# A decoder layer over 32 sequences: the order of TensorE's steps in an attention round, wide score passes first, and a selection cut into four parts

## The chip, the cores and the metric

The kernel runs on one core of one Trainium2 chip. The metric is the device time in microseconds of one execution. Three executions of the kernel before took 3460.85, 3463.48 and 3466.79 us; their median is 3463.48 us.

A core has five engines that run side by side, each through its own queue: TensorE (matmuls and transposes through PSUM; PE in the profile, with its weight loads shown as PEld), VectorE (DVE), ScalarE (ACT), GpSimd (POOL) and SyncE (SP, here the engine that issues nearly all DMAs).

## The reference

The input is 32 sequences of 256 tokens with 256 features, and for each a context of 120 rows with 256 features. Three blocks follow one another, each as x = layernorm(x + block(x)).

- Latent self-attention. A token is projected to a latent of 72 numbers, which is key and value for all 16 heads. Each head projects the token to a query of 72. The scores q·k/4 are masked causally, go through a softmax, and weigh the latents. The 16 results of 72 are put together (1152 numbers) and projected to 256.
- Cross-attention with 16 heads of 64 over the context: queries from x, keys and values from the context, softmax, output projection.
- A mixture of experts with a shared expert. A gate of 16 experts gives each token a softmax. Each expert takes the 32 highest-scored tokens of each sequence, applies a gated unit with a hidden width of 512 and adds its output, times the score, to these tokens. A shared unit of the same form runs over all tokens.

All arrays are float32.

```
scores = einsum('bhtl,bsl->bhts', q, Wdkv) / 4          # causal mask, softmax, then
y      = einsum('bhts,bsl->bhtl', attn, Wdkv)           # z @ out_w + out_b
logits = einsum('bthk,bfhk->bhft', k, q)                # cross attention, softmax, v, Wo
topk_w, topk_idx = top_k(softmax(x @ gate_w.T).T, 32)   # per sequence and expert
```

## The kernel before

**Two stages.** The attention stage does both attention blocks, sequence by sequence, in 32 calls of `attention_round(n)` (line 790). A stage of experts follows (`feed_forward`, line 1048), in whose first part the last steps of attention are mixed. The change lies in the attention stage, apart from two lines of the second.

**A round is a pipeline over sequences.** Round n works on the latent attention of sequence n, on the end of that of n-1, on the cross-attention of n-1 and n-2, on the routing of n-3, and prepares n+1. It has four sections, 0 to 3. Each begins with `scores(n, g)` (line 401) for one group g of four heads.

**Scores.** A head's 72 query numbers are split into 64 and 8. The 8s of four heads lie side by side in one tile, 32 rows a head, so `scores` runs four matmuls at a time in 32-row tiles of the array (line 410). Then the 64s of two heads run at a time in 64-row tiles (line 422). The scores of a head fill one PSUM bank of 384 columns: 128 for the first half of the tokens (the narrow pass, t = 0, which needs the first 128 keys only) and 256 for the second half (the wide pass, t = 1). A float32 matmul appears as two instructions in the profile. Afterwards VectorE adds the causal mask, which copies the scores from the bank into the tile `sm` (line 431) and frees the bank.

**Softmax and turning.** `weights(n, g, t)` (line 434) takes maxima on VectorE, four exponentials on ScalarE, reciprocals on VectorE and the product on GpSimd (line 455). `turns` transposes the weights in three steps k of four blocks (`turn`, line 457), into the banks pT; k = 0 and 2 are copied out by ScalarE, k = 1 by VectorE. A section turns the weights of the group before it: `turns(n, g-1)`, and section 0 `turns(n-1, 3)`.

**Weighing.** `weigh(s, g)` (line 480) multiplies the turned weights with the 64-wide part of the values, in tiles of 64 columns. `weigh_rest` (line 503) does the 8-wide rest of all heads in tiles of 32 columns. `latent_out` (line 520) projects to 256, adds x and normalizes.

**Cross-attention.** `cross_keys`, `cross_values` and `cross_queries` (lines 541 to 587) are projections with all 128 rows. `cross_scores(s, c0, t)` (line 589) uses 64-row tiles and fills both banks of the kind "l". `cross_weights` is the softmax over them, `cross_turn` transposes, `cross_weigh` (line 630) works in 64-column tiles, and `cross_out` (line 652) projects, adds, normalizes and stores.

**PSUM.** Of the eight banks, two have the tag "l" and six the tag "r" (`BUFS`, line 127). All other steps take an "r" bank when they begin. A new allocation takes the bank of the sixth allocation before it, and the matmul waits until that bank's reader is done. `scores` takes four banks at once.

**Routing and selection.** Every four sequences `route` and `score` compute the gate. Every eight sequences `select(g)` (line 731), at the end of section 3 of rounds 10, 18 and 26 and once in the stage of experts, transposes the scores of eight sequences by 16 experts to 128 rows of 256, and finds the 32 highest in each row. It does so four times over: the eight highest (`max`, line 745), their positions (`max_index`, line 746), and their replacement by -1 (`match_replace`, line 748). At the end of the next round `place` turns the positions into offsets.

**What sets the order.** In rounds 1 to 31 TensorE and ScalarE follow the order of the program as written; in round 0 SyncE does too. The orders of VectorE, GpSimd and SyncE come from a planner, which uses estimated costs and the order of the program as priority. Instructions under `urgent()` (line 139) come earlier in its order.

```
for n in range(1, B):
    attention_round(n)
last_section()
```

Of the kernel before, what the change touches and what calls it, by code (L numbers as in the profile page):

```python
# [20 lines left out]
F32 = mybir.dt.float32  # L21
# [5 lines left out]
P = 128  # L27
# [5 lines left out]
def decoder_kernel(  # L33
# [23 lines left out]
    nc = tc.nc  # L57
# [343 lines left out]
    def scores(s, g):  # L401
        st = states[s]
        nm = f"{st['nm']}_{g}"
        pS = [bank("r", [P, 3 * P], f"pS_{nm}_{j}") for j in range(HG)]


        for t in range(TC):
            for j in range(HG):
                rows = slice(j * 32, (j + 1) * 32)
                nc.tensor.matmul(  # L410
                    pS[j][:, SEG[t]],
                    st["q8"][rows, t * P : (t + 1) * P],
                    kr[rows, g, 0 : (t + 1) * P],
                    start=(t == 0),
                    stop=False,
                )
        for a in range(2):
            for t in range(TC):
                for odd in range(2):
                    rows = slice(odd * LM, (odd + 1) * LM)  # L420
                    k = st["kD"] if odd else st["kT"]
                    nc.tensor.matmul(  # L422
                        pS[2 * a + odd][:, SEG[t]],
                        st["qT", g][rows, a, t * P : (t + 1) * P],
                        k[rows, 0 : (t + 1) * P],
                        start=False,
                        stop=(t == TC - 1),
                    )
        sm = sp.tile([P, HG, 3 * P], F32, tag="sm", bufs=2, name=f"sm_{nm}")
        for j in range(HG):  # L430
            nc.vector.tensor_tensor(sm[:, j, :], pS[j], mask, ALU.add)  # L431
        st["sm", g] = sm

    def weights(s, g, t):

        st = states[s]
        nm = f"{st['nm']}_{g}_{t}"
        block = st["sm", g][:, :, SEG[t]]
        softmax(block, block, HG, (t + 1) * P, nm)
# [291 lines left out]
    def select(g):  # L731

        sc = scs[g]
        pst = bank("r", [P, T], f"pst_{g}")
        for t in range(TC):
            nc.tensor.transpose(
                pst[:, t * P : (t + 1) * P], sc[:, t].rearrange("p b e -> p (b e)"), ident
            )
        left = ap.tile([P, T], F32, tag="left", bufs=1, name=f"left_{g}")
        with urgent():  # L740
            nc.vector.tensor_copy(left, pst)
        idx = ap.tile([P, CAP], mybir.dt.uint32, tag="idx", bufs=1, name=f"idx_{g}")
        for k in range(CAP // 8):
            best = ap.tile([P, 8], F32, tag="best", name=f"best_{g}_{k}")
            nc.vector.max(best, left)
            nc.vector.max_index(idx[:, k * 8 : (k + 1) * 8], best, left)
            if k < CAP // 8 - 1:
                nc.vector.match_replace(
                    out=left, in_to_replace=best, in_values=left, imm_value=-1.0
                )  # L750
        at = ap.tile([P, CAP], F32, tag="at", bufs=2, name=f"at_{g}")
        nc.vector.tensor_copy(at, idx)
        nc.vector.tensor_scalar(at, at, row0, None, ALU.add)
        ats[g] = at
# [14 lines left out]
    def run(step, s, *args):  # L769
        if 0 <= s < B:  # L770
            step(s, *args)
# [5 lines left out]
    def both(step, s, *args):  # L777
        for odd in range(2):
            run(step, s, *args, odd)

    def turns(s, g):
        for k in range(3):
            run(turn, s, g, k)
# [5 lines left out]

    def attention_round(n):  # L790
        scores(n, 0)
        turns(n - 1, 3)
        both(cross_turn, n - 2, 0, 1)
        weights(n, 0, 0)
        queries(n, 1)
        run(turn_x2, n - 3)
        run(weigh, n - 1, 2)
        weights(n, 0, 1)
        run(weigh, n - 1, 3)
        run(weigh_rest, n - 1)  # L800
        if routed(n):
            route((n - 3) // BQ)
        run(cross_weigh, n - 2, 0)
        run(cross_scores, n - 2, 4, 0)
        both(cross_weights, n - 2, 4, 0)
        run(latent_out, n - 1)
        if n:
            run(load, n + 1)
            run(load_context, n + 1)

        scores(n, 1)
        run(cross_scores, n - 2, 4, 1)
        turns(n, 0)
        both(cross_turn, n - 2, 4, 0)
        weights(n, 1, 0)
        run(cross_values, n - 1, 0)
        run(cross_values, n - 1, 1)
        weights(n, 1, 1)
        run(turn_x1, n - 1)
        cross_keys(n, 0)  # L820
        if n == 0:
            out_weights(0)
        if routed(n):
            score((n - 3) // BQ)
        queries(n, 2)
        run(cross_weights, n - 2, 4, 1, 0)
        run(cross_queries, n - 1, 0, 0)
        run(cross_weights, n - 2, 4, 1, 1)
        run(cross_queries, n - 1, 0, 2)

        scores(n, 2)
        run(cross_scores, n - 1, 0, 0)
        turns(n, 1)
        both(cross_turn, n - 2, 4, 1)
        weights(n, 2, 0)
        run(turn_x, n + 1)
        run(cross_queries, n - 1, 4, 0)
        weights(n, 2, 1)
        run(cross_queries, n - 1, 4, 2)
        queries(n, 3)  # L840
        run(keys, n + 1)
        run(query_rest, n + 1)
        run(cross_weights, n - 1, 0, 0, 0)
        cross_keys(n, 1)
        run(cross_weights, n - 1, 0, 0, 1)
        if n == 0:
            load_weights([(wv_sb, wv)])
            out_weights(1)

        weigh(n, 0)  # L850
        weigh(n, 1)
        run(cross_weigh, n - 2, 4)
        scores(n, 3)
        run(cross_scores, n - 1, 0, 1)
        turns(n, 2)
        run(place_keys, n + 1)
        both(cross_turn, n - 1, 0, 0)
        weights(n, 3, 0)
        run(values, n + 1)
        run(queries, n + 1, 0)  # L860
        weights(n, 3, 1)
        both(cross_weights, n - 1, 0, 1)
        run(cross_out, n - 2)
        if n == 0:
            load_weights([(wq_sb, wq), (wo_sb, wo), (gw_sb[:, :, 0:E], gate_w)])


        if n - 3 >= BG and (n - 3) % BG == 0:
            place((n - 3) // BG - 1)
        if n - 3 >= 0 and (n - 2) % BG == 0:  # L870
            select((n - 3) // BG)

    last = B - 1

    def last_section():

        both(cross_turn, last - 1, 0, 1)
        weigh(last, 2)
        turns(last, 3)
        turn_x2(last - 2)  # L880
        weigh(last, 3)
        weigh_rest(last)
        cross_weigh(last - 1, 0)
        cross_scores(last - 1, 4, 0)
        both(cross_weights, last - 1, 4, 0)
        latent_out(last)
# [190 lines left out]

    with tc.manual_schedule(engines={mybir.EngineType.PE, mybir.EngineType.Pool}):
        fill(1)
        cross_values(last, 0)  # L1080
        cross_values(last, 1)
        cross_scores(last - 1, 4, 1)
        both(cross_weights, last - 1, 4, 1)
        both(cross_turn, last - 1, 4, 0)
        turn_x1(last)
        fill(1)
        cross_queries(last, 0, 0)
        cross_queries(last, 0, 2)
        cross_queries(last, 4, 0)
        cross_queries(last, 4, 2)  # L1090
        cross_scores(last, 0, 0)
        both(cross_weights, last, 0, 0)
        both(cross_turn, last - 1, 4, 1)
        fill(4)
        cross_weigh(last - 1, 4)
        cross_scores(last, 0, 1)
        both(cross_weights, last, 0, 1)
        both(cross_turn, last, 0, 0)
        cross_out(last - 1)
        fill(2)  # L1100
        both(cross_turn, last, 0, 1)
        fill(1)
        turn_x2(last - 1)
        fill(1)
        cross_weigh(last, 0)
        cross_scores(last, 4, 0)
        both(cross_weights, last, 4, 0)
        fill(3)
        cross_scores(last, 4, 1)
        both(cross_weights, last, 4, 1)  # L1110
        both(cross_turn, last, 4, 0)
        fill(4)
        both(cross_turn, last, 4, 1)
        fill(1)
        cross_weigh(last, 4)
        fill(1)
        cross_out(last)
        fill(3)
        turn_x2(last)
        fill(1)  # L1120
        route(last // BQ)
        fill(1)
        score(last // BQ)
        fill(3)
        select(B // BG - 1)
        fill(8)
        place(B // BG - 1)
        for _ in work:
            pass
# [52 lines left out]
```

## Time and profile before

| | us |
|---|---|
| median of three executions | 3463.48 |
| the profiled execution | 3464.54 |
| its span, first to last instruction | 3462.7 |
| TensorE busy | 3408.3 |
| VectorE busy | 1546.7 |
| ScalarE busy | 1518.9 |
| GpSimd busy | 1068.4 |
| one round (1087.69 to 1162.03) | 74.34 |
| its sections 0, 1, 2, 3 | 24.25, 16.49, 19.20, 14.40 |

The granted clock of TensorE was 0.996 of full speed over the span. A section is counted from the first matmul of its scores to that of the next. The rounds from the third to the last take 74.33 to 75.64 us, but for those that follow a selection (77.78, 77.55 and 77.43 us) and those after them (75.0 us).

A line of the profile gives the engine, the line of the kernel, the operation, the tiles written and read, the shapes, and how many there are. In a timeline the first two numbers are the start and the length in us; a bracket at the end gives how long the engine stood idle before and who ended that. A line with "x16" joins sixteen neighbours. Matmuls overlap: the distance between starts, not the length of one, is what one costs. Busy time of TensorE therefore counts much that isn't dense work.

### The profile page before, as it was taken

How to read it: one execution, taken by the hardware profiler on the slowest of the kernel's cores; microseconds unless marked ns; L12 is line 12 of the kernel's file. 1: busy time of each engine (PE TensorE's matmuls, PEld its weight loads, DVE VectorE, ACT ScalarE, POOL GpSimd, SP SyncE). 2: the span in 40 equal slices, each digit the busy share in tenths (PEclk: the TensorE clock that was granted, in tenths of full speed). 3: DMA queues.
4: the chain of work that ended last, by engine and by line, in shares of the span. 5: the costliest groups of instructions: out<-in, count | busy, mean ns of one | idle time of the engine just before them, and what ended most of it. 6: DMA issues, size and time to landing. Idle time of an engine off the chain costs nothing.

```text
span 3462.7 us, 60611 instructions
## 1 busy us (share of the span) xinstructions
PE 3408.3 (98%) x23516; PEld 2546.7 (74%) x23516; DVE 1546.7 (45%) x3416; ACT 1518.9 (44%) x5458; POOL 1068.4 (31%) x947
## 2 busy tenths in 40 slices
PE   8999999999999999999999999999999999999999
PEld 6787788887788888778888878887666656666655
DVE  4555455555545545555555554553311133221133
ACT  4655555655555555555555555554311111111111
POOL 3323223323222332222332323233444411444410
PEclk9999999999999999999999999999999999999999
DMA  3000000000000000000000000002455532455421
GB/s 97 9 17 22 20 20 18 18 18 16 26 16 22 16 18 18 22 20 19 19 17 18 17 25 16 19 13 78 108 123 124 132 97 61 117 123 123 105 82 52
DMA packets 142614, 164.58 MB, mean 48 GB/s; under 512 B 29432, under 2 KB 118264, under 8 KB 142328
## 3 DMA queue, kind: packets, MB, share of 16 engines
q1 hardware_dynamic: 117536, 126.08, 12.2%
q0 software_dynamic: 24576, 34.62, 5.7%
q8 instruction: 187, 3.06, 0.4%
q14 instruction: 99, 0.81, 0.1%
q10 hardware_dynamic: 216, 0.01, 0.0%
HBM read 105.61 MB, written 50.86 MB: 45 GB/s over the span
## 4 chain that ended last, share of the span: by engine, by line
PE 94%; DVE 3%; POOL 1%; ACT 1%; DMA 0%; issue 0%; SPq 0%; POOLq 0%; DVEq 0%; ACTq 0%
PE po L180 14%; PE pq L180 7%; PE pqx L180 6%; PE pd L180 6%; PE pu L180 6%; PE pg L180 6%; PE pz L489 5%; PE pT L469 5%; PE pS L422 4%; PE pL L596 3%; PE pxT L622 3%; PE pc L638 3%; PE pkx L180 3%; PE pu_s L180 3%; PE pg_s L180 3%; PE pfo L180 3%
## 5 line engine op out<-in xcount | busy, mean ns | idle before, releaser
L455 POOL TENSOR_TENSOR sm<-sm,rs 128x512 f32<-128x512 f32 (+1 forms) x256 | 375.3, 1466 | 956.4 <-DVE rs L454 950.9
L447 ACT ACTIVATE sm<-sm,nmax 128x128 f32<-128x128 f32 (+1 forms) x1024 | 452.5, 446 | 9.1 <-DVE nmax L444 8.9
L475 ACT COPY pt<-pT 128x512 f32<-128x512 f32 x256 | 150.1, 586 | 661.0 <-PE pT L469 661.0
L455 POOL TENSOR_TENSOR xsm_x<-xsm_x,rs_x 128x480 f32<-128x480 f32 x256 | 251.1, 986 | 399.5 <-DVE rs_x L454 373.8
L447 ACT ACTIVATE xsm_x<-pL,nmax_x 128x120 f32<-128x120 f32 x1024 | 354.1, 372 | 43.2 <-DVE nmax_x L444 43.2
L981 POOL DMA_INDIRECT acc<-eo,offs x128 | 200.8, 1568 | 322.3 <-DVE eo L978 292.9
L431 DVE TENSOR_TENSOR sm<-pS,mask 128x384 f32<-128x384 f32 x512 | 249.9, 548 | 93.4 <-PE pS L422 93.0
L180 PE MATMUL pq<-xT,wd_sb 128*128 128x256 f32 x1152 | 282.8, 387 | 1.9 <-DVE wd_sb L266 1.9
L180 PE MATMUL po<-ow_sb,zT 128*128 128x256 f32 x1152 | 257.2, 382 | 0.0
L180 PE MATMUL pu<-xeT,wu 128*128 128x512 f32 x512 | 241.9, 595 | 0.0
L180 PE MATMUL pg<-xeT,wg 128*128 128x512 f32 x512 | 240.7, 592 | 0.0
L180 PEld LDWEIGHTS po<-ow_sb,zT 128*128 128x128 f32 x1152 | 216.2, 190 | 31.9 <-issue 0.2
L180 PEld LDWEIGHTS pq<-xT,wd_sb 128*128 128x128 f32 x1152 | 215.8, 194 | 30.3 <-DVE wd_sb L266 2.7
L1045 DVE TENSOR_TENSOR hT<-gl,pu 128x512 f32<-128x512 f32 x128 | 87.9, 687 | 334.9 <-PE pu L180 254.8
L444 DVE TENSOR_REDUCE nmax<-sm 128x4 f32<-128x512 f32 (+1 forms) x256 | 234.7, 947 | 4.2
L469 PE MATMUL pT<-ident,sm 128*128 128x128 f32 x1536 | 204.0, 279 | 29.5 <-DVE sm L431 19.0
L154 POOL TENSOR_TENSOR rstd<-rstd,mhalf 128x2 f32<-128x2 f32 (+1 forms) x97 | 67.1, 692 | 536.9 <-DVE rstd L153 536.9
L180 PE MATMUL pqx<-x1T,wq_sb 128*128 128x256 f32 x1024 | 232.5, 380 | 0.0
L180 PE MATMUL pd<-wd,hT 128*128 128x256 f32 x1024 | 226.3, 379 | 0.0
L180 PE MATMUL po<-wo_sb,cxT 128*128 128x256 f32 x1024 | 226.2, 379 | 0.0
L447 ACT ACTIVATION_READ_ACCUMULATOR xsm_x<-pL,nmax_x 128x1 f32 x1024 | 225.0, 220 | 0.0
L180 PEld LDWEIGHTS po<-wo_sb,cxT 128*128 128x128 f32 x1024 | 194.4, 190 | 26.8 <-issue 0.5
(136 smaller groups left out, 6031.6 us busy)
## 6 DMA issues: line engine op xcount, KB each, us to landing
wg<-in_wg_dram SPq DMA_DIRECT2D x32, 512.0 KB
wu<-in_wu_dram SPq DMA_DIRECT2D x32, 512.0 KB
wd<-in_wd_dram SPq DMA_DIRECT2D x32, 512.0 KB
x<-in_x_dram SPq DMA_DIRECT2D x32, 256.0 KB
rows<-x SPq DMA_DIRECT2D x32, 256.0 KB
acc<-x SPq DMA_DIRECT2D x32, 256.0 KB
x2t<-x2T SPq DMA_DIRECT2D x32, 256.0 KB
fx2T_s<-x2t SPq DMA_DIRECT2D x16, 512.0 KB
```

The source lines that it names most:

```text
L180: nc.tensor.matmul(acc, lhsT, rhs, start=(i == 0), stop=(i == n - 1))
L422: nc.tensor.matmul(pS[2 * a + odd][:, SEG[t]], st["qT", g][rows, a, t * P : (t + 1) * P], k[rows, 0 : (t + 1) * P], start=False, stop=(t = ...
L431: nc.vector.tensor_tensor(sm[:, j, :], pS[j], mask, ALU.add)
L444: nc.vector.tensor_reduce(nmax, src, AX.X, ALU.max, negate=True)
L447: nc.scalar.activation(dst[:, a, :], src[:, a, :], AF.Exp, bias=nmax[:, a : a + 1], accum_out=rs[:, a, :],)
L455: nc.gpsimd.tensor_tensor(dst, dst, rs.to_broadcast([P, n, width]), ALU.mult)
L469: nc.tensor.transpose(pT[:, j, :], block, ident)
L475: nc.scalar.copy(dst, pT)
L489: nc.tensor.matmul(pz[odd * LM : (odd + 1) * LM, a, k * P :], st["v"][:, k, 0:LM], moving(st, g, 2 * a + odd, k), start=(k == 0), stop=(k ...
L596: nc.tensor.matmul(pLs[odd][:, j, :], st["qxT", c0][rows, j, t * P : (t + 1) * P], st["kxT"][rows, c0 + j, :], start=True, stop=True,)
L622: nc.tensor.transpose(pT[:, j, :], st["xsm", c0, t, odd][:, j, :], ident)
L981: nc.gpsimd.indirect_dma_start(out=acc[b], out_offset=self.rows(b), in_=eo[:, k, :], in_offset=None, compute_op=ALU.add,)
```

## The change

1. In `scores` the wide pass (t = 1) goes ahead of the narrow one, both among the 32-row matmuls and among the 64-row ones. The start flag moves to the wide pass, the stop flag to the narrow one.
2. In each section a cross step follows the scores ahead of the turns. `cross_scores(n-2, 4, 0)` moves from in front of `latent_out` to directly behind the scores of section 0, as cross scores already stand in the other sections. Then comes a projection: half of `cross_values` in sections 0 and 1 (before, both halves stood in section 1), `cross_queries(n-1, 4, 0)` in section 2, and `queries(n+1, 0)` in section 3.
3. In section 0 `weigh_rest` goes ahead of the two `weigh` steps. Half of `cross_keys` moves from the end of section 2 into section 3. Some `weights` and `cross_weights` change places with these steps, which changes ScalarE's order.
4. `select` finds the first eight only. A new function `choose(g, k)` finds the others, one eight at the end of each of sections 0 to 2 of the next round (`best_of`). In the stage of experts all four still follow one another.
5. `cross_values(31, 0)` moves from the stage of experts to the beginning of the last section.

```diff
-        for t in range(TC):
+        wide = range(TC - 1, -1, -1)
+        for t in wide:
             for j in range(HG):
...
-                    start=(t == 0),
+                    start=(t == TC - 1),
...
-            for t in range(TC):
+            for t in wide:
...
-                        stop=(t == TC - 1),
+                        stop=(t == 0),
...
+        ats[g] = left, idx
+        choose(g, 0)
+
+    def choose(g, k):
+        left, idx = ats[g]
+        best = ap.tile([P, 8], F32, tag="best", name=f"best_{g}_{k}")
+        nc.vector.max(best, left)
+        nc.vector.max_index(idx[:, k * 8 : (k + 1) * 8], best, left)
+        if k < CAP // 8 - 1:
+            nc.vector.match_replace(out=left, in_to_replace=best, in_values=left, imm_value=-1.0)
+            return
...
     def attention_round(n):
         scores(n, 0)
+        run(cross_scores, n - 2, 4, 0)
+        run(cross_values, n - 1, 0)
         turns(n - 1, 3)
         both(cross_turn, n - 2, 0, 1)
         weights(n, 0, 0)
         queries(n, 1)
         run(turn_x2, n - 3)
+        weights(n, 0, 1)
+        run(weigh_rest, n - 1)
         run(weigh, n - 1, 2)
-        weights(n, 0, 1)
         run(weigh, n - 1, 3)
-        run(weigh_rest, n - 1)
         if routed(n):
             route((n - 3) // BQ)
         run(cross_weigh, n - 2, 0)
-        run(cross_scores, n - 2, 4, 0)
         both(cross_weights, n - 2, 4, 0)
         run(latent_out, n - 1)
...
+        best_of(n, 1)
 
         scores(n, 1)
         run(cross_scores, n - 2, 4, 1)
+        run(cross_values, n - 1, 1)
         turns(n, 0)
         both(cross_turn, n - 2, 4, 0)
         weights(n, 1, 0)
-        run(cross_values, n - 1, 0)
-        run(cross_values, n - 1, 1)
+        cross_keys(n, 0)
         weights(n, 1, 1)
         run(turn_x1, n - 1)
-        cross_keys(n, 0)
...
+        best_of(n, 2)
 
         scores(n, 2)
         run(cross_scores, n - 1, 0, 0)
+        run(cross_queries, n - 1, 4, 0)
         turns(n, 1)
         both(cross_turn, n - 2, 4, 1)
         weights(n, 2, 0)
         run(turn_x, n + 1)
-        run(cross_queries, n - 1, 4, 0)
+        run(cross_queries, n - 1, 4, 2)
         weights(n, 2, 1)
-        run(cross_queries, n - 1, 4, 2)
         queries(n, 3)
         run(keys, n + 1)
+        run(cross_weights, n - 1, 0, 0, 0)
         run(query_rest, n + 1)
-        run(cross_weights, n - 1, 0, 0, 0)
-        cross_keys(n, 1)
         run(cross_weights, n - 1, 0, 0, 1)
...
+        best_of(n, 3)
 
         weigh(n, 0)
         weigh(n, 1)
         run(cross_weigh, n - 2, 4)
         scores(n, 3)
         run(cross_scores, n - 1, 0, 1)
+        run(queries, n + 1, 0)
         turns(n, 2)
         run(place_keys, n + 1)
         both(cross_turn, n - 1, 0, 0)
+        both(cross_weights, n - 1, 0, 1)
+        cross_keys(n, 1)
         weights(n, 3, 0)
         run(values, n + 1)
-        run(queries, n + 1, 0)
         weights(n, 3, 1)
-        both(cross_weights, n - 1, 0, 1)
         run(cross_out, n - 2)
...
+    def best_of(n, k):
+        if n - 3 >= BG and (n - 3) % BG == 0:
+            choose((n - 3) // BG - 1, k)
...
     def last_section():
+        cross_values(last, 0)
         both(cross_turn, last - 1, 0, 1)
...
-        cross_values(last, 0)
         cross_values(last, 1)
...
         select(B // BG - 1)
+        for k in range(1, CAP // 8):
+            choose(B // BG - 1, k)
```

More of the change, by code (lines that the diff above doesn't have):

```diff
@@ L742, in select @@
         idx = ap.tile([P, CAP], mybir.dt.uint32, tag="idx", bufs=1, name=f"idx_{g}")
[L743 to L750, printed above, removed]
+        ats[g] = left, idx
[8 more added lines that the diff above has]
+            return
         at = ap.tile([P, CAP], F32, tag="at", bufs=2, name=f"at_{g}")
```

## Prediction

> **What bounds the kernel now.** I read the page's busy shares and its chain first, then TensorE's own waits, then the timeline of one round in the steady state, from 1087.69 to 1162.03 us. The page, its first section and the head of its fourth:
>
> ```profile
> PE 3408.3 (98%) x23516; PEld 2546.7 (74%) x23516; DVE 1546.7 (45%) x3416; ACT 1518.9 (44%) x5458; POOL 1068.4 (31%) x947
> ...
> PE 94%; DVE 3%; POOL 1%; ACT 1%; DMA 0%; issue 0%; SPq 0%; POOLq 0%; DVEq 0%; ACTq 0%
> ```
>
> TensorE is 94% of the chain, in an order written by hand. A moved step can only pay by ending a wait of TensorE or by letting its stream run denser. The waits, restricted to TensorE (us in total, times, longest):
>
> ```profile
> PE pT L469 <- DVE sm L431: 19.0, 27, 1.5
> PE pT L469 <- POOL sm L455: 6.9, 3, 2.3
> ...
> PE pT L469 <- DVE offs L762: 3.6, 3, 1.2
> ```
>
> About once a round the turning of weights (pT) waits for VectorE's mask addition (sm). The timeline shows why:
>
> ```profile
> 1087.69 0.94 PE L410 MATMUL pS<-kr,q 32*128 32x128 f32 x16
> 1087.80 0.69 DVE L662 TENSOR_TENSOR r<-po,x 128x512 f32<-128x512 f32 x1 [0.94 <-PE po L180]
> ...
> 1088.56 0.37 PE L422 MATMUL pS<-kT,qT 64*128 64x128 f32 x1
> ...
> 1088.78 0.27 PE L422 MATMUL pS<-kT,qT 64*128 64x128 f32 x1
> ...
> 1090.07 1.09 PE L469 MATMUL pT<-ident,sm 128*128 128x128 f32 x8
> ...
> 1091.17 1.94 DVE L431 TENSOR_TENSOR sm<-pS,mask 128x384 f32<-128x384 f32 x4
> ...
> 1091.77 0.66 PE L469 MATMUL pT<-ident,sm 128*128 128x128 f32 x4 [0.60 <-DVE sm L431]
> ```
>
> Six PSUM banks go round. Section 0's scores take four, the first two turns the last two, and the third turn needs the bank of the first scores. VectorE, busy with cross_out's normalization, frees it only at about 1091.7. In section 1 the same twelve transposes take 1.37 us (1115.20 to 1116.57); here 2.26 (1090.07 to 1092.33). The wait costs 0.89 us a round.
>
> The second loss is at changes of tile shape. Two 256-wide matmuls just after one, then three in mid-stream:
>
> ```profile
> 1103.76 0.28 PE L596 MATMUL pL<-kxT,qxT 64*128 64x120 f32 x2
> 1103.97 0.70 PE L180 MATMUL po<-ow_sb,zT 128*128 128x256 f32 x2
> ...
> 1104.29 0.81 PE L180 MATMUL po<-ow_sb,zT 128*128 128x256 f32 x3
> ```
>
> Mid-stream they start 0.216 apart (2 x 0.216 + 0.38 = 0.81). After the change the second starts 0.32 after the first: 0.10 more. The first itself comes 0.21 after a 120-wide matmul that streams for 0.103: 0.10 more again. So an entry into 128-column weights costs about 0.20 us. From the same round's starts, into 64 columns (pz, pc) it costs 0.10 + 0.05, into 32 (pzr) 0.10 + 0.02, into transposes 0.10 + 0.056.
>
> **What the Trainium skill says.** TensorEngine Tiling (Array Packing), Key Properties: changing the tiling mode drains TensorE. The trace agrees: 0.093 to 0.113 us each. TensorE: Matmul & The Clock Gate, LDWEIGHTS: a load lasts columns/1.2 ns, 107, 53 and 27 ns for 128, 64 and 32 columns. The trace's second delays, 104, 51 and 24 ns, look like exactly one exposed load. PSUM — Partial Sum Buffer, The four PSUM rules: a start clears the flags of a whole bank, so one start on the wide pass serves the narrow one too; no trace line prices this. The same page, Engine vs sequencer instructions: ScalarE's and VectorE's queues are strict first in, first out; the trace's copies behind exponentials agree.
>
> **The change part by part.**
>
> *Wide passes first.* Same matmuls; the first after each of two entries (32-row, 64-row) becomes 256 wide instead of 128. If its longer stream hid the second load, 0.104 us would go, 2 x 128 times: 26.6 us. In 64-row and 32-row tiles the trace has only narrow firsts (1088.56 to 1088.78: 0.22 for a 0.109 stream), equal to either reading. But the wide firsts elsewhere, po at 256 above and pg after a change at 512, still pay 0.104. Bounds: 0 to 26.6 us gained, and a loss is excluded because the loads are the same. I take 0, by the wide rows.
>
> *Cross scores and values behind section 0's scores.* Cross scores use 64 rows as the latent ones do: no entry. cross_values' half adds 4 x 0.429 = 1.72 us ahead of the turns. From the section's start: scores 2.28 (0.868 + 1.414, section 1), cross scores 0.98 to 3.26, values with their entry 1.83 to 5.09, first turn to 5.53. The values take the fifth bank, so the second turn now needs the bank freed at 1091.71 - 1087.69 = 4.02. Margin 1.5 us: the 0.89 goes. cross_values is taken from section 1, so its stream costs nothing; its ScalarE copy (0.5 us) comes with it.
>
> *Order of the weighing.* Before, section 0 enters 64 columns, 32, 64, 64 rows and 128: 0.144 + 0.124 + 0.164 + 0.203 + 0.209 = 0.844 us. After: 32, 64, 128: 0.117 + 0.164 + 0.204 = 0.485. Gain 0.36; in the 7 rounds with routing (32 columns between) five entries stay and 0.07 is gained. weigh_rest is now first and needs turn 3's copies, which by the same count end over 1 us before it (VectorE's near 8, weigh_rest at 9.5).
>
> *What follows the scores.* In all four sections a projection instead of transposes follows the shape change: 0.104 instead of 0.056 exposed. Loss 4 x 0.048 = 0.19.
>
> *Moved steps on ScalarE.* Queries, keys and cross weights change places in its hand order; a round holds 41.9 us of ScalarE work in 74.3, so only local lateness counts. The tightest place is section 3's scores, whose third bank is freed by the zT copy:
>
> ```profile
> 1145.06 0.61 ACT L501 COPY zT<-pz 128x512 f32<-128x512 f32 x1
> ...
> 1147.63 0.94 PE L410 MATMUL pS<-kr,q 32*128 32x128 f32 x16
> ```
>
> Now 1.96 us early. cross_keys' half (1.87 us of TensorE) leaves the stretch ahead, so TensorE arrives sooner: at 17.5 us from section 2's start. ScalarE: keys copied by 12.7 (TensorE ends them at 12.2), four-plus-four exponentials at 1.4 us each and the q8 copy 0.4 to 15.8, zT copy to 16.4. Margin 1.1 us: cost 0. The other banks, traced the same way, have 0.8 us or more. VectorE's, GpSimd's and SyncE's orders are the planner's and I cannot see them: the same additions, maxima and copies, with the DMAs of loads, stores and placed keys kept in their sections. kr's four DMAs still have over 12 us to land.
>
> *Selection by eights.* Three rounds now run four rounds of maxima (0.42), index (0.09 + 0.42) and replacement (0.09 + 0.41) on VectorE between the scores' additions, with two short conversions: about 6.4 us. Section 0 lasts 27.57, 27.35 and 27.23 there instead of 24.25, the excess mostly waiting and then matmuls at half rate after the idle (four transposes take 1.08 us, where 0.60 is usual). After, one set of 1.4 us and the 0.41 copy remain there; its first addition then frees a bank near 4.5 to 4.9, before the 5.53 that TensorE needs. The other three sets go behind sections 0 to 2, where VectorE is idle 4 us at a time. Gain 9.4. The eight offset copies (8 x 0.16) cost 24.91 - 24.25 = 0.66 in the next round; the new margin covers them: 2.0 in all.
>
> *First rounds.* Rounds 1 and 2 wait 2.5 and 2.4 us at the same turns, for GpSimd, and lose about 2 more to the half rate. Values of 1.83 us ahead cover most: about 4, between 0 and 6. The value weights are asked for at 21.6 us and not needed before 53. The tail's moved step is neutral.
>
> Sum: ordinary rounds 0.89 + 0.36 - 0.19 = 1.05 x 22 = 23.1; routed rounds 0.89 + 0.07 - 0.19 = 0.77 x 7 = 5.4; selection 9.4 + 2.0; first rounds 4. Together 44. I keep 4 back for the planner's unseen orders (0.13 a round): 40. The profiled execution took 3464.5 us (span 3462.7) and so becomes 3424.5; it lies 1 us above the median of 3463.48. Forecast 3424.
>
> **Rivals.**
>
> *The load hides behind a wide first.* For: LDWEIGHTS overlaps matmuls mid-stream. Against: the 256- and 512-wide firsts. It adds 26.6: 3397.
>
> *The wait only moves.* The planner puts other VectorE work ahead of the additions, or copies free banks late. For: its order on VectorE already put indices between additions. Against: 1.5 us of margin and a VectorE half idle. If half of the 0.89 stays and selection keeps half its cost: 31 x 0.44 + 5.7 = 19 lost, 3443.
>
> *ScalarE becomes the gate at section 3's scores*, the case of the other sign. Two cross-weight groups stand ahead of the zT copy. Each us that ScalarE is late beyond the 1.1 costs a us in some 31 rounds; the gain of about 42 is used up at 1.35 us of stall, so from 2.5 us of lateness the kernel is slower. At 3 us of lateness: 31 x 1.9 = 59, less 40: 3482. For: the cross weights fall directly ahead of it in a first-in-first-out queue. Against: the count, and ScalarE's 44%.
>
> **How the numbers follow.** Main case (3410 to 3436) 0.56; hidden load 0.12; wait moves 0.16; no visible difference 0.06, if the planner takes all back; slower 0.10. A measurement tells 0.2%, 7 us, from no change. The first three are faster: 0.84. For eight in ten, 3392 to 3450 takes in most of the hidden-load and wait-moves cases and leaves out slower, equal and some of the latter's end.
>
> **What would show it.** Right: no sm wait of TensorE in section 0; ordinary rounds near 73.2 instead of 74.34; scores still 2.28 us; select rounds within 0.5 of the others. If scores fall to 2.07, the load hides. Wrong: rounds over 74.3 with TensorE at a pS or pL bank that a ScalarE copy or VectorE addition frees.

## The result, and the profile after

The changed kernel takes 3423.09 us (median of four, 3422.8 to 3423.94), against 3462.16 for the kernel before (median of four). The ratio is 0.9886, with a 95% interval from 0.9869 to 0.9903. Forecast were 3424 us, and a main case from 3410 to 3436. The profiled execution has a span of 3421.4 us, 41.3 less than the 3462.7 before. That is more than the 39.1 between the medians, because the profiled execution of the kernel before (3464.54) lay 2.4 above its median.

The page of the changed kernel, its first section and the head of its fourth. TensorE's busy time falls by 21.7 us; the other half of the gain is idle time, 34.8 us of the span instead of 54.4:

```profile
PE 3386.6 (99%) x23516; PEld 2569.9 (75%) x23516; DVE 1549.0 (45%) x3416; ACT 1491.7 (44%) x5458; POOL 1071.0 (31%) x947
...
PE 96%; DVE 2%; ACT 1%; POOL 1%; DMA 0%; issue 0%; SPq 0%; POOLq 0%; DVEq 0%
```

TensorE's own waits in the changed kernel (us in total, times, longest). The 27 waits of pT for the mask addition are gone. So are those for the offsets. Three new ones of 1.3 us each have come, of the rest of the weighing (pzr) for a copy of turned weights (pt), and one in the tail has grown from 1.2 to 3.0:

```profile
PE pT L470 <- POOL sm L456: 5.9, 3, 2.3
...
PE pzr L511 <- DVE pt L474: 4.0, 3, 1.3
...
PE px1T L170 <- DVE x L156: 3.0, 1, 3.0
```

Section 0 of a steady round in the timeline, from 1068.09 on. VectorE adds the mask no sooner than before (3.47 us after the section's start, 3.48 before). But TensorE now has cross scores and values in between and reaches the turns at 5.07 instead of 2.38 us. The twelve transposes run as one block:

```profile
1068.09 0.94 PE L411 MATMUL pS<-kr,q 32*128 32x256 f32 x16
1068.20 0.69 DVE L663 TENSOR_TENSOR r<-po,x 128x512 f32<-128x512 f32 x1 [1.27 <-PE po L180]
...
1070.37 1.05 PE L597 MATMUL pL<-kxT,qxT 64*128 64x120 f32 x16
...
1071.35 1.98 PE L180 MATMUL pvx<-wv_sb,c 128*120 128x512 f32 x4
1071.56 1.95 DVE L432 TENSOR_TENSOR sm<-pS,mask 128x384 f32<-128x384 f32 x4
1073.16 1.47 PE L470 MATMUL pT<-ident,sm 128*128 128x128 f32 x12
```

The busy time by section, changed kernel first, then the kernel before (columns: stretch, its length, then busy us and instructions of PE, PEld, DVE, ACT, POOL, granted clock, DMA share, GB/s):

```profile
1068.09:1092.79 24.70, 24.70 (x233) 19.42 (x233) 11.28 (x25) 10.77 (x41) 6.42 (x6) 1.00 0.10 34
1092.79:1107.54 14.75, 14.75 (x117) 12.49 (x117) 9.67 (x22) 8.90 (x34) 3.88 (x4) 1.00 0.11 28
1107.54:1125.01 17.47, 17.47 (x154) 14.47 (x153) 10.64 (x21) 11.67 (x49) 8.04 (x8) 1.00 0.03 7
1125.01:1141.24 16.23, 16.23 (x129) 14.53 (x127) 7.04 (x16) 9.69 (x39) 4.09 (x4) 1.00 0.01 3
```

```profile
1087.69:1111.94 24.25, 23.65 (x230) 18.35 (x229) 11.22 (x25) 10.38 (x40) 5.85 (x6) 1.00 0.10 33
```

Section 0 is 0.45 us longer although 1.83 us of values came into it; the other sections shift by what moved between them. The round is 73.15 us instead of 74.34, 1.19 less. Over the kernel, taken from the starts of the rounds in both traces:

| part | before | after | gain, us |
|---|---|---|---|
| an ordinary round | 74.34 | 73.15 | 1.19 |
| a routed round | 75.42 | 74.52 | 0.90 |
| section 0 after a selection | 27.57, 27.35, 27.23 | 26.09, 26.09, 26.10 | 1.48, 1.26, 1.13 |
| the same, above an ordinary section 0 | 9.40 in all | 4.18 in all | 5.2 |
| the round after that, section 0 above ordinary | 0.66 each | 0.19 each | 1.4 in all |
| rounds 0 to 2 | 173.37 | 169.03 | 4.3 |

The first scores start 0.6 us later in the second trace (15.27 instead of 14.68), and what follows the start of the last section 3 is 1.6 us longer, that section's own shift taken off. With these two the parts add up to the 41.3.

Not all of it is shorter waits. The trace also records the clock that TensorE was granted. In the kernel before it stood at half of full speed for 3.4 us in each of the three sections 0 after a selection (from 791.9, 1392.6 and 1993.4) and once in round 1 (from 54.6). In these stretches TensorE's starts lay twice as far apart, 0.21 us instead of 0.109 and 0.43 instead of 0.216. Counted by these starts, they cost about 4.4 us after the selections and 1.7 us in round 1. One of them, with the clock in the column after POOL:

```profile
791.90:795.30 3.40, 3.38 (x10) 2.89 (x11) 3.40 (x10) 1.05 (x4) 0.00 (x0) 0.50 0.02 5
```

The changed kernel's trace has no such stretch before its tail. So by this count some 6 of the 41.3 us are clock; no ordinary round is touched by it.

### The profile page after: what moved, and what is told of

It reads as the page before. It is cut to its first block, busy times and chain, and to the rows that moved or that the text cites. A ratio compares the mean times of both kernels' runs of the same rounds, so it can differ in the third digit from the quotient of the medians.

```text
span 3421.4 us, 60519 instructions
## 1 busy us (share of the span) xinstructions
PE 3386.6 (99%) x23516; PEld 2569.9 (75%) x23516; DVE 1549.0 (45%) x3416; ACT 1491.7 (44%) x5458; POOL 1071.0 (31%) x947
## 4 chain that ended last, share of the span: by engine, by line
PE 96%; DVE 2%; ACT 1%; POOL 1%; DMA 0%; issue 0%; SPq 0%; POOLq 0%; DVEq 0%
PE po L180 14%; PE pq L180 7%; PE pqx L180 7%; PE pu L180 6%; PE pd L180 6%; PE pg L180 6%; PE pS L423 5%; PE pz L490 5%; PE pT L470 5%; PE pc L639 3%; PE pkx L180 3%; PE pg_s L180 3%; PE pu_s L180 3%; PE pL L597 3%; PE pfo L180 3%; PE pxT L623 3%
## 5 line engine op out<-in xcount | busy, mean ns | idle before, releaser
L566 ACT COPY vx<-pvx 120x512 f32<-120x512 f32 x64 | 37.5, 586 | 509.7 <-PE pvx L180 509.7
L180 PE MATMUL pqx<-x1T,wq_sb 128*128 128x256 f32 x1024 | 241.9, 385 | 0.0
L180 PEld LDWEIGHTS pqx<-x1T,wq_sb 128*128 128x128 f32 x1024 | 191.3, 192 | 27.3
L180 PEld LDWEIGHTS pd<-wd,hT 128*128 128x128 f32 x1024 | 192.4, 190 | 25.6 <-issue 1.0
```

Source lines behind the costliest of these rows:

```text
L180: nc.tensor.matmul(acc, lhsT, rhs, start=(i == 0), stop=(i == n - 1))
```

## The experiments

The parts were undone or done alone. A steady round repeats to 0.01 us within a trace, so small parts are read from rounds and sections, and medians serve as a check.

**Narrow passes first again.** Does the order of the two passes have a share?

```diff
-        wide = range(TC - 1, -1, -1)
+        wide = range(TC)
...
-                    start=(t == TC - 1),
+                    start=(t == 0),
...
-                        stop=(t == 0),
+                        stop=(t == TC - 1),
```

> The changed kernel with the narrow passes first again, start and stop flags with them; all else stays. Theory (after an entry into another tile shape the second weight load is exposed whatever the width of the first matmul, so the order of the passes is worth nothing): a steady round stays at 73.15 us within 0.05, a section's scores at 2.28, the total within 3 us of the changed kernel's 3423. Rival (the wide pass first has a part in the gain, by hiding a load or by freeing banks sooner): scores 2.3 to 2.5, a round 73.5 to 74.0, the total 3433 to 3450.

Measured: 3423.77 us (0.988, 0.9864 to 0.9897), an ordinary round of 73.16, section 0 at 24.70. Two timelines show why. With the narrow pass first, the second matmul of the 64-row block starts 0.21 us after the first:

```profile
1070.60 0.37 PE L423 MATMUL pS<-kT,qT 64*128 64x128 f32 x1
...
1070.81 0.27 PE L423 MATMUL pS<-kT,qT 64*128 64x128 f32 x1
```

With the wide pass first, in the changed kernel, 0.32 us after:

```profile
1068.95 0.48 PE L423 MATMUL pS<-kT,qT 64*128 64x256 f32 x1
...
1069.27 0.38 PE L423 MATMUL pS<-kT,qT 64*128 64x256 f32 x1
```

The streams are 0.109 and 0.216 us; 0.104 is left over in both. So a wider first matmul hides nothing of what the second one waits for. Only round 2 differed, by 1.66 us. Its turns wait 2.02 us in this run and 2.03 in the changed kernel for the weights that GpSimd multiplies. Behind that wait, the next 16 transposes started at 0.21 us intervals in this run and at 0.109 in the changed kernel's. The granted clock explains it; this run, then the changed kernel, in the same 3.4 us:

```profile
116.90:120.30 3.40, 3.40 (x16) 3.40 (x17) 2.10 (x4) 0.59 (x1) 0.00 (x0) 0.50 0.00 0
```

```profile
116.90:120.30 3.40, 3.25 (x23) 3.10 (x24) 2.73 (x5) 1.84 (x6) 0.09 (x1) 1.00 0.00 0
```

Why the clock fell behind one of two equal waits stays open; the order of the passes is not shown to be the cause.

**Cross scores alone.** The kernel before, with one line moved.

```diff
         scores(n, 0)
+        run(cross_scores, n - 2, 4, 0)
         turns(n - 1, 3)
...
-        run(cross_scores, n - 2, 4, 0)
         both(cross_weights, n - 2, 4, 0)
```

> The kernel before with one step moved: the cross scores of section 0 go from in front of latent_out to directly behind that section's scores. Theory (0.98 us of cross scores ahead of the turns is about what the wait needs, and one entry of tile shape goes with them): section 0 from 24.25 to 23.15 us (0.89 of wait and 0.21 of entries less; up to 0.1 of wait may stay), a steady round 73.2 to 73.35, in all 32 to 36 us less than before, near 3428. Rival (the half of cross_values is what ends the wait): half of the wait or more stays, a round of 73.7 or over, a gain of 20 us or less.

Measured: 3432.77 us (0.9906, 0.9889 to 0.9922), 32.6 less than the kernel before, whose median, taken alongside, was 3465.34. Section 0 has 23.17 us, a round 73.26. The turns run through, and the first addition begins 0.2 us after the first transpose, soon enough for the third turn, which needs the bank that it frees:

```profile
1077.63 0.94 PE L410 MATMUL pS<-kr,q 32*128 32x128 f32 x16
...
1079.91 1.05 PE L596 MATMUL pL<-kxT,qxT 64*128 64x120 f32 x16
...
1080.89 1.53 PE L469 MATMUL pT<-ident,sm 128*128 128x128 f32 x12
...
1081.10 1.95 DVE L431 TENSOR_TENSOR sm<-pS,mask 128x384 f32<-128x384 f32 x4
```

The steady part is as expected, and so is the gain. The total is 5 us above the guess of 3428, in good part because round 2 took 79.32 us instead of 75.99. There the cross scores now wait 1.98 and 0.88 us for ScalarE, which has not yet read their banks, and from 118.1 on the granted clock is at half for 6.8 us.

```profile
PE pL L596 <- ACT xsm_x L447: 2.9, 2, 2.0
```

So this one moved line brings 32.6 of about 40 us (39.1 by the medians, 41.3 by the spans).

**The order of the weighing undone**, in the changed kernel.

```diff
-        weights(n, 0, 1)
-        run(weigh_rest, n - 1)
         run(weigh, n - 1, 2)
+        weights(n, 0, 1)
         run(weigh, n - 1, 3)
+        run(weigh_rest, n - 1)
```

> The changed kernel with the old order of the weighing in section 0: weigh 2, exponentials, weigh 3, weigh_rest. Theory: one more entry of 64 columns in ordinary rounds, section 0 from 24.70 to 24.85 us; one less in routed rounds, from 25.85 to 25.71. In the three rounds after a selection weigh_rest comes 2.65 us later, so its wait for VectorE's copy of a turn goes: section 0 there from 26.09 to about 24.9. Total 3419 to 3424. Rival (the first place of weigh_rest matters by more than entries): a steady round differs by over 0.3 us.

Measured: 3423.8 us (0.9884, 0.9868 to 0.9901). Section 0 has 24.85 in ordinary rounds and 25.71 in routed ones, both as expected: entries of tile shape add up as counted. The third expectation was wrong. After a selection section 0 has 26.25, not 24.9; the wait has passed to the step that now comes first:

```profile
PE pz L490 <- DVE pt L474: 4.0, 3, 1.3
```

weigh 2 doesn't read that copy; it belongs to the next group. So the wait is for a PSUM bank: in both kernels the first weighing step, whichever it is, starts when VectorE's copy has freed the bank of the second turn. Changing places among steps that take their banks in the same order doesn't help.

**The selection in one piece again**, in the changed kernel.

```diff
         ats[g] = left, idx
-        choose(g, 0)
+        for k in range(CAP // 8):
+            choose(g, k)
```

with `best_of` left empty, and the loop at the last selection gone.

> The changed kernel with the selection in one piece again, all four eights at the end of rounds 10, 18 and 26. Theory (formed on the changed kernel's trace: the planner had put all four eights of the split selection into section 0 of the next round anyway): the rounds after a selection keep 74.65 us within 0.3, section 0 there 26.1 within 0.3, the total is the changed kernel's within 2 us. Rival (the forecast's own step, that the split keeps three of four sets out of section 0): section 0 there 27.5 or more, the total 4 to 9 us longer.

Measured: 3420.36 us (0.9871, 0.9855 to 0.9888). Section 0 after a selection has 25.40 us, 0.7 less than with the split, where 26.1 within 0.3 had been expected; all other rounds are equal. So the split gains nothing and costs some 2 us. VectorE's timeline of the changed kernel in that section, which begins at 772.44, shows all four sets of maxima within 13 us of it:

```profile
774.01 0.39 DVE L751 MAX8 best<-left 128x8 f32<-128x256 f32 x1
...
776.47 0.42 DVE L751 MAX8 best<-left 128x8 f32<-128x256 f32 x1
...
782.29 0.41 DVE L751 MAX8 best<-left 128x8 f32<-128x256 f32 x1
782.62 0.67 DVE L474 COPY pt<-pT 128x512 f32<-128x512 f32 x1
...
784.71 0.43 DVE L751 MAX8 best<-left 128x8 f32<-128x256 f32 x1
```

The four calls stand in four sections of the program, but VectorE's order is the planner's. It set the three later ones into section 0 too, where their inputs are ready. The copy that TensorE waits for ends at 783.29; pzr starts at 783.35.

In this run, with the selection in one piece, that wait is gone, though the copy comes no sooner:

```profile
782.46 2.81 PE L511 MATMUL pzr<-pt,v 128*32 128x256 f32 x64
...
782.97 0.68 DVE L474 COPY pt<-pT 128x512 f32<-128x512 f32 x1
```

pzr starts ahead of the copy, so here it has another bank than the second turn's. The rule that a bank is that of the sixth allocation before doesn't hold in this place; how the banks are given out when VectorE's order changes stays open. In place of the 1.3 us two cross turns wait 0.3 us each for the mask additions.

**Cross scores and order of weighing, nothing else**, on the kernel before: the diffs of the second experiment and the third, the latter the other way round.

> The kernel before with two parts of the change: the cross scores of section 0 behind its scores, and weigh_rest ahead of the two weigh steps. No projection stands between scores and turns, and the selection is in one piece. Theory: the run with the cross scores alone had 73.26 us a round; one 64-column entry less gives 73.11, and 0.14 more in routed rounds; sections 1 to 3 stay at 16.49, 19.20 and 14.40. A steady round then equals the changed kernel's 73.15 without any projection behind the scores. Total near 3430, because the first rounds (63.0 and over 75 us) and the rounds after a selection (about 75.2) keep what the projections cover. Rival (the projections carry part of the steady gain): a round of 73.4 or more.

Measured: 3427.95 us (0.9897, 0.9882 to 0.9912; 3424.65 to 3432.72). An ordinary round has 73.11 us, a routed one 74.47, and sections 1 to 3 are unchanged. In the steady state two small moves do as well as the whole change, 0.04 us better. The projections behind the scores pay only elsewhere: the round after a selection has 75.22 here and 74.65 in the changed kernel, the next one 73.77 and 73.34, and rounds 1 and 2 61.39 and 76.23 against 59.62 and 74.96.

**The first turn ahead of the projection**, in the changed kernel, in all four sections.

```diff
         run(cross_scores, n - 2, 4, 0)
+        run(turn, n - 1, 3, 0)
         run(cross_values, n - 1, 0)
-        turns(n - 1, 3)
+        run(turn, n - 1, 3, 1)
+        run(turn, n - 1, 3, 2)
```

> The changed kernel with the first of the three turns ahead of the projection in all four sections, so that transposes again follow the change of tile shape. Theory (a transpose's exposed load is 0.056 us, a projection's 0.104): each section 0.04 to 0.05 us shorter, a steady round 72.96 to 73.0, the total 5 to 6 us less than 3423, near 3417. Rival (a projection behind the scores costs nothing, or the earlier turn waits for its weights): a round of 73.1 or more.

Measured: 3417.17 us (0.9861, 0.9846 to 0.9876), an ordinary round of 72.98; the sections have 24.66, 14.71, 17.42 and 16.19, each 0.04 to 0.05 less. As expected. One wait is new: in the second round behind a selection, values wait 0.33 us for the offset copies, and section 0 has 25.22 there instead of 24.89.

**The selection in front of latent_out**, in the changed kernel, in one piece and a section later.

```diff
+        if n - 3 >= BG and (n - 3) % BG == 0:
+            select((n - 3) // BG - 1)
         run(latent_out, n - 1)
...
-        if n - 3 >= 0 and (n - 2) % BG == 0:
-            select((n - 3) // BG)
```

> The changed kernel with the whole selection moved from the end of rounds 10, 18 and 26 to the next round, in front of latent_out's 8 us of matmuls, where VectorE is idle. Theory (VectorE's 6.4 us of selection are worth what they delay of the copies that TensorE needs, and there they delay none): section 0 after a selection 24.9 us (24.70 and the two transposes), against 26.09 with the split and 25.40 in one piece; total 3 to 4 us less than 3423. Rival (the selection then delays the normalization behind latent_out and TensorE waits in section 1): section 1 of these rounds over 15.2 us.

Measured: 3419.62 us (0.9869, 0.9854 to 0.9884). Section 0 after a selection has 24.88 us, the 24.70 of an ordinary one and about what two transposes take; section 1 stays at 14.75. VectorE's timeline shows the selection done by 796.2, and 1.31 us of idle time left before the addition that follows latent_out:

```profile
789.75 0.42 DVE L742 COPY left<-pst 128x256 f32<-128x256 f32 x1 [0.53 <-PE pst L737]
...
795.97 0.24 DVE L759 TENSOR_SCALAR at<-at,row 128x32 f32<-128x32 f32 x1
797.52 0.69 DVE L531 TENSOR_TENSOR r<-po,x 128x512 f32<-128x512 f32 x1 [1.31 <-PE po L180]
```

What a planner can't be told by the place of a call, it is told by a dependence: the two transposes on TensorE are in the hand-written order, and VectorE's work can't begin before them.

**The two together, and the routing matmuls behind weigh_rest**, in the changed kernel.

```diff
         run(weigh_rest, n - 1)
+        if routed(n):
+            route((n - 3) // BQ)
         run(weigh, n - 1, 2)
         run(weigh, n - 1, 3)
-        if routed(n):
-            route((n - 3) // BQ)
```

> The changed kernel with both of these, the first turn ahead of the projection and the selection in front of latent_out, and the routing matmuls directly behind weigh_rest, so that the two steps of 32 columns share an entry. Theory: a steady round 72.96 to 73.0, a routed one 0.29 us less on top (two entries, 0.124 + 0.164), rounds after a selection near 73.3; in all 5.5 + 3.5 + 2 = 11 us less than 3423, near 3412. Rival (the gains lean on the same slack and do not add): 3416 or more.

Measured: 3411.62 us (0.9846, 0.9832 to 0.9859), 11.5 less than the changed kernel's median and 11.8 less by the spans. An ordinary round has 72.98 us; section 0 of a routed round 25.53 instead of the 25.81 of the sixth experiment; a round after a selection 73.27. The gains add. The wait of 0.33 us in three rounds that came with the sixth experiment stays.

## Why the prediction was right, and where its steps were not

**The wait in section 0.** Right. The forecast had the bank free 4.02 us after the section's start and the second turn at 5.53. The trace has the first addition end near 4.0 (it begins at 3.47, and one takes 0.54) and the second turn near 5.5. It overlooked that the cross scores alone, at 0.98 us, would do: the second experiment shows it, and the fifth that no projection is needed in the steady state.

**Wide passes first.** Right: 0 us. The rival of the hidden load falls with the first experiment.

**Entries of tile shape.** Right to the hundredth: 0.15 us for the order of weighing in the third experiment, and 0.04 to 0.05 a section for projections in the place of transposes, in the sixth.

**The ordinary round.** It was to lose 1.05 us and lost 1.19. Short waits around the cross turns of sections 0 and 1, about 0.05 us in each, went as well and had not been counted. Ordinary and routed rounds so gave 22 x 1.19 + 7 x 0.90 = 32.5, not 28.5.

**ScalarE's copy at section 3.** Right. The zT copy ends 1.23 us before the scores that need its bank; 1.1 had been counted. The rival of the other sign had no ground here.

```profile
1123.18 0.60 ACT L502 COPY zT<-pz 128x512 f32<-128x512 f32 x1
1125.01 0.93 PE L411 MATMUL pS<-kr,q 32*128 32x256 f32 x16
```

**Selection by eights.** Wrong in its mechanism. The step said that three sets go behind sections 0 to 2, and that the first addition then frees its bank in time, for 9.4 us. The gain was 5.2, and none of it is from the split: the sets never left section 0, and in one piece the rounds are shorter by 0.7. The waits for the mask additions (1.5, 0.3 and 0.2 us) did go, because cross scores and values now stand ahead of the turns. But in their place came a wait of 1.3 us for another bank, behind VectorE's copy of a turn, for which no margin had been counted. Waits account for only about 0.8 of the 5.2 us. The other 4.4 are the stretches at half clock, which the changed kernel's trace no longer has. In the second experiment, too, these sections ran at full clock, with waits of 0.6, 0.3 and 0.2 us left. The offset copies gave 1.4 of the 2.0 us.

**First rounds.** 4.3 us, 4 had been said, but not by the mechanism that was named. The values were to cover most of the two waits for GpSimd. These only went from 2.34 to 1.50 and from 2.22 to 2.03 us, so about 1.0 us. The larger single part, 1.7 us, is the stretch at half clock that is gone from round 1. Whether it comes can differ between two runs with equal waits, as the first experiment shows, so the number was right in part by luck.

**The tail.** "Neutral" was near, but not exact. Half of the values had covered the normalization behind the last latent_out; TensorE's wait there went from 1.23 to 2.95 us, while two waits of 0.46 and 0.34 us in the last section went. What follows the start of the last section 3 is some 1.6 us longer after that section's own shift of 1.83 is taken off. One execution says little here: the third experiment has the same tail, and its trace 1116.2 us from there on, where the changed kernel's has 1118.9.

**The total.** Against the sum of 44 us the rounds gave 4.0 more and the first rounds 0.3 more. The selection gave 4.2 less, the offset copies 0.6 less, the tail cost 1.6 and the later start 0.6; that makes 41.3. The 4 us kept back for the planner happened to cover the difference. What was named and right, the wait in section 0 and the entries, carries most of the gain; that the total fits to about 1 us is in part luck.

## What to carry to other kernels

Where a hand-ordered engine waits for a buffer, look for a step that uses other buffers and the tile shape already in force; moved there it can end the wait and save an entry of shape. One such line gave most of this gain. Count changes of tile shape as instructions with a price, and choose what follows a change by its weight load. A call that was split and spread in the program was not spread on VectorE, whose order a planner makes; tying it to an instruction whose place is fixed did it. Before a gain or loss is put down to waits, look at the granted clock of the same stretch.

## What the runs showed of the hardware

After a change of tile shape the second matmul comes late: by 0.104 us for weights of 128 columns, behind a first matmul of 109, 216 or 429 ns alike, although mid-stream no such delay is seen. The delay is 0.051 us for 64 columns, 0.024 for 32 and 0.056 for transposes. The weight loads that the trace of the kernel before records for these four last 190, 137, 110 and 141 ns on average, each about 86 more than its delay. So we read it as a weight load in the open. With the drain of 0.093 to 0.113 us an entry costs about 0.2 us for 128 columns and 0.12 for 32. A steady round of the changed kernel holds 16 of them in its 73 us, some 3 us; one of the kernel before had 18.

Short waits can be followed by a slower clock. In the stretches found in the attention stage the granted clock stood at half for 3.4 us, once for 6.8. They came at the end of idle stretches of only some 2 us, or shortly behind them: 2.34 us in round 1 of the kernel before; 1.5, 0.3 and 0.2 us in its sections after a selection; 2.02 us in round 2 of the first experiment; 1.98 and 0.88 us in round 2 of the second. Behind nearly equal waits it stayed at full speed: 2.22 us in round 2 of the kernel before, 2.03 us there in the changed kernel, 1.98 and 0.88 us there in the fifth experiment. What decides it these runs don't show. A wait so can cost up to 1.7 us more than its own length, or 3 in the second experiment, and a single round is no measure of a change.
